# A quarter of the columns ahead in a Householder loop, side work laid out anew: a subspace rotation followed by a DiT block

## The chip, the cores and the metric

The kernel runs on one core of one Trainium2 chip, in fp32 throughout. The metric is the device time of one execution in microseconds (us); the time of a kernel is the median of several runs. Times inside an execution come from one profiled execution, counted from the start of its span. Engines are named as the profile names them: PE is TensorE's matmul (PEld its weight load), DVE is VectorE, ACT ScalarE, POOL GpSimd, SP SyncE, which issues most DMAs.

## The reference

The kernel computes two layers. The first rotates every token inside a 64-dimensional subspace; the second is a DiT block. With batch 8, 512 tokens of width 576:

```
U, _ = qr(P)                                   # P is 576 x 64, U has orthonormal columns
v = silu(cond) @ W.T + b                       # 2016 entries per batch element
A = skew(v);  R = expm(A)                      # 8 matrices of 64 x 64
z = x @ U
x = x + (z @ R - z) @ U.T                      # the rotation

ada = silu(cond) @ ada_w + ada_b               # shifts, scales, gates: 6 x 576 per batch element
x = x + gate_msa * attention(modulate(layernorm(x), shift_msa, scale_msa))   # 16 heads, over heads of one token
x = x + gate_mlp * mlp(modulate(layernorm(x), shift_mlp, scale_mlp))         # 576 -> 2304 -> gelu -> 576
```

Only what comes before the first token matters here: the QR of P, the matrices expm(A), and the products for `ada`.

## The kernel before

**The whole.** The kernel starts with a prologue of about 240 us and then runs the tokens in blocks of 128 through rotation, qkv, attention, projection and MLP for the remaining 1900 us, which this change doesn't touch. The prologue factors P by Householder reflections. Once the 64 reflections are known, the code after the loop (from L571) forms v^T v (`vv`, L577), inverts a triangular 64x64 matrix by levels (`p1`, `p2t`), and makes from that U, U^T and the first rotated block of tokens. All of that needs the whole factorization, and the blocks of tokens need it too.

**The matrix.** P lies in SBUF as `m`, 128 partitions x 5 row blocks x 64 columns; row j of the matrix (j below 64) is partition j of block 0. Step j works on the n = 64 - j columns from j on; n is how this text counts steps, 64 for the first one, 1 for the last.

**One step (`qr_step`, `column_products`).** The work of a step alternates between TensorE, ScalarE and VectorE:

- `rp` (L274): a TensorE product with a broadcast column of the identity copies row j of the matrix to all partitions. It reads row j of all remaining columns, so it needs all of the previous step's update.
- `dp` (L282): a product with a matrix of ones sums `t` over the partitions: the dot products of column j with each remaining column. `t` (L268) are sums over the five row blocks of the products `pr` (L263), made by the previous step.
- VectorE: `sg` (L291) is 0 or -2 by the sign of the diagonal entry in `rp`; `off` (L292) clears row j's place in `m`; `row` (L295) is (sg + 1) times row j. ScalarE: `nrm` (L298) is the root of column j's dot product, `nsg` (L299) is sg + 1.
- `w` (L320) = row x nrm - dp; `den` (L323) = (nrm - row_j) x nrm; `r` (L335) is its reciprocal; `up` (L327) is column j times `w`; `m` (L337) adds r x up. Then `pr` and `t` for the next step.
- `finish` makes `av` = nrm - row_j (L306), `vmax`, the largest entry of column j (L307), and `dg`, the diagonal correction (L310). The correction itself (L311) is put into the next step by `done`.

The instructions `up`, `m`, `pr` and `t` are cut into two halves of the columns (`halves`, h=0 and h=1) as long as at least 16 columns are left, in the order pr0, pr1, t0, t1.

**The side work (`beside`, L528).** After each step from the third on, one piece of other work is put into the engines' streams. The pieces come from generators:

- `skew_entries` (L399): 8 groups of 5 matmuls, the entries of A; with `paced(4, ...)` four matmuls a step. Then A is written to DRAM and read back as matrices (`skew_rows`).
- `modulations` (L517): 9 groups of 5 matmuls of `ada` (`ada_columns`, L360, six passes for three of them), and after four of the groups a `modulation` (L371), 10 or 12 small passes. `paced(3, ...)` makes it three a step.
- `expm` (L445): the products of a Taylor series in A (at, aa, ss, sss, hic, hin, sn), then 19 squarings (L503), each of two 16-pass products `pe` and `pf` of 64x64 matrices (the last has one only), a copy on ScalarE and an addition on POOL (L513); its result is `fmi` (L515).

In `beside` each yield of `expm` says whether the step is free: then three more matmuls of `ada` go with it. A squaring says False, so a pair has its step to itself. By this, skew lies at n=60 to 51, `ada` with the head of expm from there to n=34, the squarings at n=33 to 16 and nothing of it from n=15 on.

**What sets the order.** PE, DVE, ACT and POOL run in the order in which the code issues (`manual_schedule`, L164); the program compiled from it holds that order[...]. The first load of `aw`, the weights of `ada`, are four groups deep (bufs=4); later groups are loaded when an earlier one has been used. The gates of the block are stored to DRAM (`gates_d`) when groups 4 and 8 are done.

## Time and profile before

| what | value |
|---|---|
| three runs | 2156.01, 2156.08, 2163.45 us; median 2156.08 |
| profiled execution | 2157.38 us, its span 2155.7 us |
| granted TensorE clock, mean over the span | 0.962 |
| first `nrm` (n=64), `nrm` of n=40, n=22, n=4 | 7.2, 93.8, 154.9, 202.5 us |
| last diagonal correction, `vv` | 210.4, 210.6 us |
| store of the first rotated rows | 233.8 us |
| from one `nrm` to the next, us | n=64: 3.90; n=60: 4.50; n=55: 3.40; n=50: 3.27; n=46: 3.11; n=45: 4.33; n=40: 4.67; n=34: 2.97; n=24: 2.91; n=16: 2.91; n=10: 2.45; n=3: 2.30 |
| `nrm`, `nsg` on ScalarE | 0.26, 0.28 us |
| `rp`, `dp` result, at full clock (n=48) | 0.42, 0.39 us |

How to read the page and the views: the busy table gives for each engine its busy time and the share of the span. The page's digits cut the span into 40 slices of 53.9 us, each digit the busy tenths of its slice; the row PEclk gives in the same way the clock that TensorE was granted. A timeline line has the start, the duration, engine, line of code, operation, names of output and inputs, shapes, and a count when equal neighbours are put together. A busy-time-by-stretch line has the stretch and its length, then for PE, PEld, DVE, ACT and POOL the busy time with the number of instructions, then the granted clock, the DMA share and GB/s.

### The profile page before, as it was taken

Reading aid. Unit: us, or ns where it says so; the run is one execution under the profiler, and the core shown is the slowest. Engines: PE = TensorE matmul, PEld = TensorE weight load, DVE = VectorE, ACT = ScalarE, POOL = GpSimd, SP = SyncE. Lnnn points to the kernel's source line nnn. Section 1 sums busy time; section 2 is a strip of 40 time slices with the busy share of each in tenths; the row PEclk is TensorE's granted clock in tenths of the full one; section 3 lists DMA queues with packets and bytes.
Section 4 is the critical chain, followed back from the end, with each engine's and each line's share of the span. In section 5 each row is a group of like instructions: output and inputs, shape, how many; then the busy total and the mean of one; then the engine's idle time right before and its main releaser. Section 6 shows DMA issues by size and latency. Waiting matters only on the chain.

```text
span 2155.7 us, 28203 instructions
## 1 busy us (share of the span) xinstructions
PE 2052.0 (95%) x10091; PEld 1622.7 (75%) x10091; DVE 1818.0 (84%) x2544; ACT 433.6 (20%) x1040; POOL 731.8 (34%) x959
## 2 busy tenths in 40 slices
PE   6996998999999999999999999999999999999988
PEld 3475666777878888787878787888878778787867
DVE  8998499799997988979797979797988998986920
ACT  2232121212111111221121212111221121112110
POOL 2341143241523333333333242423333443343422
PEclk9965799999999999999999999999999999999989
DMA  8202265385857666565758484857667666665744
GB/s 278 87 2 75 85 209 164 114 234 161 225 178 223 194 191 222 174 217 178 234 143 271 133 266 127 244 176 210 213 180 234 187 210 182 200 189 193 218 129 131
DMA packets 251456, 392.44 MB, mean 182 GB/s; under 512 B 86926, under 2 KB 139099, under 8 KB 251316
## 3 DMA queue, kind: packets, MB, share of 16 engines
q1 hardware_dynamic: 225396, 364.09, 55.3%
q10 hardware_dynamic: 25920, 26.55, 3.6%
q8 instruction: 80, 1.31, 0.2%
q14 instruction: 60, 0.49, 0.1%
HBM read 331.63 MB, written 58.94 MB: 181 GB/s over the span
## 4 chain that ended last, share of the span: by engine, by line
PE 77%; DVE 12%; issue 3%; DMA 3%; POOL 3%; ACT 1%; ACTq 0%; SPq 0%; POOLq 0%; DVEq 0%
PE fc L993 25%; PE qkvp L821 17%; PE fc L1067 9%; PE pj L949 6%; PE fc L1072 6%; PE p L1097 3%; PE fc L1069 3%; DVE sc L866 2%; DVE qk L859 1%; DVE pv L887 1%; PE zps L751 1%; DVE att L894 1%; PE rot L762 1%; PE dp L282 1%; PE htr L794 1%
## 5 line engine op out<-in xcount | busy, mean ns | idle before, releaser
L993 PE MATMUL fc<-h2T,w 128*128 128x256 f32 x2304 | 521.1, 382 | 3.3 <-ACT h2T L969 2.1
L821 PE MATMUL qkvp<-wqkv,hT 128*128 128x288 f32 (+1 forms) x1920 | 486.5, 410 | 8.6 <-ACT qs L832 6.4
L993 PEld LDWEIGHTS fc<-h2T,w 128*128 128x128 f32 x2304 | 434.7, 191 | 71.7 <-ACT h2T L969 9.1
L821 PEld LDWEIGHTS qkvp<-wqkv,hT 128*128 128x128 f32 (+1 forms) x1920 | 364.3, 192 | 111.4 <-ACT qs L832 8.2
L859 DVE TENSOR_TENSOR qk<-qkv 128x2304 f32<-128x2304 f32 x128 | 336.8, 2631 | 15.3 <-DMA qkv<-tok 11.1
L887 DVE TENSOR_TENSOR pv<-sc,qkv 128x2304 f32<-128x2304 f32 x128 | 332.5, 2598 | 2.7
L894 DVE TENSOR_REDUCE att<-pv 128x144 f32<-128x2304 f32 x128 | 325.9, 2546 | 3.1
L866 DVE TENSOR_REDUCE sc<-qk 128x64 f32<-128x2304 f32 x128 | 326.0, 2547 | 2.5
L1092 POOL TENSOR_TENSOR s<-gt 128x128 f32<-128x128 f32 x144 | 93.5, 651 | 461.8 <-ACT gt L1014 461.8
L1014 ACT ACTIVATE gt<-fc,b 128x256 f32<-128x256 f32 x288 | 118.9, 472 | 604.5 <-PE fc L993 570.1
L1067 PE MATMUL fc<-wq,gt 128*128 128x288 f32 x576 | 170.5, 416 | 10.1 <-ACT gt L1014 7.5
L1072 PEld LDWEIGHTS fc<-wt,ss 128*128 128x128 f32 x1152 | 160.6, 190 | 15.1
L1072 PE MATMUL fc<-wt,ss 128*128 128x144 f32 x1152 | 164.7, 286 | 0.0
L832 ACT COPY qs<-qkvp 128x288 f32<-128x288 f32 x180 | 71.7, 398 | 377.0 <-PE qkvp L821 325.0
L1025 POOL TENSOR_TENSOR x<-x,mt 128x288 f32<-128x288 f32 x64 | 71.3, 1114 | 221.7 <-DVE mt L1024 221.7
L1089 POOL TENSOR_TENSOR ss<-gt 128x128 f32<-128x128 f32 x144 | 121.1, 841 | 65.1 <-PE fc L1072 65.0
L1091 POOL TENSOR_TENSOR ss<-gt,ss 128x128 f32<-128x128 f32 x144 | 130.5, 907 | 10.0
L1067 PEld LDWEIGHTS fc<-wq,gt 128*128 128x128 f32 x576 | 99.4, 190 | 44.5 <-issue 15.9
L949 PE MATMUL pj<-w2q_p,aT 128*128 128x288 f32 x384 | 105.2, 410 | 0.8 <-DVE u L1117 0.8
L146 POOL TENSOR_TENSOR rstd_m<-rstd_m,mhalf 128x1 f32<-128x1 f32 x32 | 24.5, 764 | 224.5 <-DVE rstd_m L145 224.5
L1067 PE MATMUL fc<-wt,gt 128*128 128x288 f32 x288 | 93.5, 406 | 0.0
L1069 PE MATMUL fc<-wq,ss 128*128 128x288 f32 x288 | 93.4, 406 | 0.0
(262 smaller groups left out, 2371.5 us busy)
## 6 DMA issues: line engine op xcount, KB each, us to landing
w<-in_fc_w SPq DMA_DIRECT2D x288, 256.0 KB, 5.0
wq<-in_fc_q SPq DMA_DIRECT2D x144, 432.0 KB, 4.3
wt<-comb_d SPq DMA_DIRECT2D x144, 432.0 KB, 5.9
tok<-qs ACTq DMA_DIRECT2D x180, 144.0 KB, 1.8
qkv<-tok SPq DMA_DIRECT2D x30, 864.0 KB, 4.6
w2q_p<-in_proj_w SPq DMA_DIRECT2D x32, 432.0 KB, 4.1
xT<-in_x_t SPq DMA_DIRECT2D x16, 640.0 KB, 4.8
w1t<-in_fc_t SPq DMA_DIRECT2D x80, 128.0 KB, 4.4
```

What stands on the lines that cost most here:

```text
L821: nc.tensor.matmul(ps, lhsT=hT[0:k, c, i * 128 : (i + 1) * 128], rhs=wqkv[0:k, c, cols], start=c == 0, stop=c == NK - 1,)
L859: nc.vector.tensor_tensor(pr, q[:, c * HC : (c + 1) * HC].unsqueeze(2).to_broadcast([128, HC, H, DH]), k.unsqueeze(1).to_broadcast([128, H ...
L866: nc.vector.tensor_reduce(sc[t][:, c * HC : (c + 1) * HC, :], pr, AX.X, ALU.add)
L887: nc.vector.tensor_tensor(pr, sc[t][:, c * HC : (c + 1) * HC, :].unsqueeze(2).to_broadcast([128, HC, DH, H]), v.unsqueeze(1).to_broadcast( ...
L894: nc.vector.tensor_reduce(att[:, c * HC : (c + 1) * HC, :], pr, AX.X, ALU.add)
L949: nc.tensor.matmul(ps, lhsT=aT[0:k, c, :], rhs=w, start=c == 0, stop=c == NK - 1)
L993: nc.tensor.matmul(bank[:, k], lhsT=lhs, rhs=h2T[rows, c, 0 : NU * 128], start=start, stop=stop, skip_group_check=True)
L1067: nc.tensor.matmul(p[k], lhsT=whole[k][0], rhs=whole[k][1], start=g == 0, stop=stop)
L1069: nc.tensor.matmul(p[2], lhsT=whole[2][0], rhs=whole[2][1], start=g == 0, stop=stop)
L1072: nc.tensor.matmul(bank[:, side], lhsT=lhs, rhs=rhs[:, n * QUARTER : (n + 1) * QUARTER], start=False, stop=stop, skip_group_check=True,)
L1089: nc.gpsimd.tensor_tensor(ss[:, 0], gt[:, 0, 1], gt[:, 1, 1], ALU.add)
L1091: nc.gpsimd.tensor_tensor(ss[:, 2], gt[:, 1, 0], ss[:, 1], ALU.subtract)
```

## The change

The change rewrites the step and its order, and lays out the side work anew. In words:

1. `halves` becomes `split`: the first quarter of the columns from lo on, then the other three quarters (one part if fewer than 16 are left). Each part has tiles of its own for `t` and for `dp` (`t0`, `t1`, `dp0`, `dp1`), so `dp` is two matmuls in a two-part step; the tile `dp1` takes one more PSUM bank.
2. The order of VectorE in a step: sg, row, off, w of the first part, w of the second, both `up`, r, m of the first part, vmax, pr of the first, m of the second, t of the first, pr and t of the second.
3. `av` is made by ScalarE, from row_j with `nrm` as bias and scale -1. In steps whose next one has two parts, `den` is made by ScalarE too, from `av` with `nrm` as scale. `nsg` goes.
4. `sg` and `av` of each step are kept as columns of `sgs` and `avs`; the corrections of the diagonal are made by three VectorE operations after the last step, in place of `dg` and the correction in each.
5. `skew_entries` is paced by two a step rather than four; `ada` by two a step for five steps, then with each yield of `expm` one, or two where it is free and its number is odd. A squaring now has one `ada` matmul (or a modulation) with it. In the compiled order: skew at n=60 to 41, two `ada` each at n=40 to 36, the head of expm with one or two at n=35 to 23, the squarings with one each at n=22 to 5, the last single product at n=4, the last `ada` at n=2. The second store of the gates is issued on SP behind the last group's copy, so at the end of the loop, and the loads issued behind it on that queue (weights of the sums, of fc1 and of the projection) come after it.

```diff
@@ -243,32 +243,33 @@
         vmax = prep.tile([128, R], F32, tag="vmax", name="vmax")
-
-        def halves(lo):
-            n = R - lo
-            if n < 16:
-                return [(lo, R)]
-            return [(lo, lo + n // 2), (lo + n // 2, R)]
+        avs = prep.tile([128, R], F32, tag="avs", name="avs")
+        sgs = prep.tile([128, R], F32, tag="sgs", name="sgs")
+        def split(lo):
+            first = lo + (R - lo) // 4
+            return [(lo, R)] if R - lo < 16 else [(lo, first), (first, R)]
         def wide(n):
             return [128, NK, n]
-        def column_products(j):
-
-            t = qrs.tile([128, R], F32, tag="t", name=f"t_{j}")
-            prods = []
-            for h, (a, b) in enumerate(halves(j)):
-                pr = qrs.tile(wide(R), F32, tag=f"pr{h}", name=f"pr_{j}_{h}", bufs=1)
-                nc.vector.tensor_tensor(
-                    pr[:, :, a:b], m[:, :, a:b], m[:, :, j : j + 1].to_broadcast(wide(b - a)), ALU.mult
-                )
-                prods.append(pr)
-            for pr, (a, b) in zip(prods, halves(j)):
-                nc.vector.tensor_reduce(t[:, a:b], pr[:, :, a:b].rearrange("p c i -> p i c"), AX.X, ALU.add)
+        def product(j, k, a, b):
+            pr = qrs.tile(wide(R), F32, tag=f"pr{k}", name=f"pr_{j}_{k}", bufs=1)
+            nc.vector.tensor_tensor(pr[:, :, a:b], m[:, :, a:b], m[:, :, j : j + 1].to_broadcast(wide(b - a)), ALU.mult)
+            return pr
+        def summed(j, k, a, b, pr):
+            t = qrs.tile([128, R], F32, tag=f"t{k}", name=f"t_{j}_{k}")
+            nc.vector.tensor_reduce(t[:, a:b], pr[:, :, a:b].rearrange("p c i -> p i c"), AX.X, ALU.add)
             return t
-        def qr_step(j, t, done):
+        def qr_step(j, ts):
             rp = ps_qr.tile([128, R], F32, tag="rp", name=f"rp_{j}")
             nc.tensor.matmul(
@@ -278,66 +279,75 @@
                 start=True,
                 stop=True,
             )
-            dp = ps_qr.tile([128, R], F32, tag="dp", name=f"dp_{j}")
-            nc.tensor.matmul(dp[:, j:R], lhsT=ones, rhs=t[:, j:R], start=True, stop=True)
-
-            def small(tag):
-                return qrs.tile([128, 1], F32, tag=tag, name=f"{tag}_{j}")
+            dps = []
+            for k, (t, (a, b)) in enumerate(zip(ts, split(j))):
+                dp = ps_qr.tile([128, R], F32, tag=f"dp{k}", name=f"dp_{j}_{k}")
+                nc.tensor.matmul(dp[:, a:b], lhsT=ones, rhs=t[:, a:b], start=True, stop=True)
+                dps.append(dp)
+            def small(tag, n=1):
+                return qrs.tile([128, n], F32, tag=tag, name=f"{tag}_{j}")
             n = R - j
-            row, sg, nsg, nrm, av = (small(x) if x != "row" else None for x in ("row", "sg", "nsg", "nrm", "av"))
-            row = qrs.tile([128, R], F32, tag="row", name=f"row_{j}")
+            row, nrm, den, r = small("row", R), small("nrm"), small("den"), small("r")
+            sg, av = sgs[:, j : j + 1], avs[:, j : j + 1]
             nc.vector.tensor_scalar(sg, rp[:, j : j + 1], 0.0, -2.0, ALU.is_ge, ALU.mult)
+            nc.vector.scalar_tensor_tensor(
+                row[:, j:R], sg.to_broadcast([128, n]), 1.0, rp[:, j:R], ALU.add, ALU.mult
+            )
             nc.vector.tensor_tensor(
                 m[:, 0, j:R], m[:, 0, j:R], off[:, j : j + 1].to_broadcast([128, n]), ALU.mult
             )
-            nc.vector.scalar_tensor_tensor(
-                row[:, j:R], sg.to_broadcast([128, n]), 1.0, rp[:, j:R], ALU.add, ALU.mult
-            )
-            nc.scalar.activation(nrm, dp[:, j : j + 1], AF.Sqrt, bias=tiny)
-            nc.scalar.activation(nsg, sg, AF.Identity, bias=ones[:, 0:1])
-            if done:
-                done()
-
-            def finish():
-
-                dg = small("dg")
-                nc.vector.tensor_scalar(av, nrm, row[:, j : j + 1], None, ALU.subtract)
+            nc.scalar.activation(nrm, dps[0][:, j : j + 1], AF.Sqrt, bias=tiny)
+            nc.scalar.activation(av, row[:, j : j + 1], AF.Identity, bias=nrm, scale=-1.0)
+            def largest():
                 nc.vector.tensor_reduce(
                     vmax[:, j : j + 1], m[:, :, j], AX.X, ALU.max, apply_absolute_value=True
                 )
-                nc.vector.tensor_scalar(dg, ident[:, j : j + 1], av, nsg, ALU.mult, ALU.mult)
-                return lambda: nc.vector.tensor_tensor(
-                    m[:, 0, j : j + 1], m[:, 0, j : j + 1], dg, ALU.subtract
-                )
-
+            cols = split(j + 1)
+            if len(cols) == 1:
+                largest()
             if j + 1 == R:
-                return None, finish()
-
-            w = qrs.tile([128, R], F32, tag="w", name=f"w_{j}")
-            den, r = small("den"), small("r")
-            nc.vector.scalar_tensor_tensor(
-                w[:, j + 1 : R], row[:, j + 1 : R], nrm, dp[:, j + 1 : R], ALU.mult, ALU.subtract
-            )
-            nc.vector.tensor_scalar(den, nrm, row[:, j : j + 1], nrm, ALU.subtract, ALU.mult)
-            outer = []
-            for h, (a, b) in enumerate(halves(j + 1)):
-                up = qrs.tile(wide(R), F32, tag=f"up{h}", name=f"up_{j}_{h}", bufs=1)
+                return None
+            if len(cols) == 1:
+                nc.vector.tensor_scalar(den, nrm, row[:, j : j + 1], nrm, ALU.subtract, ALU.mult)
+            else:
+                nc.scalar.activation(den, av, AF.Identity, scale=nrm)
+            w = small("w", R)
+            for dp, (a, b) in zip(dps, split(j)):
+                a = max(a, j + 1)
+                if a < b:
+                    nc.vector.scalar_tensor_tensor(w[:, a:b], row[:, a:b], nrm, dp[:, a:b], ALU.mult, ALU.subtract)
+            def outer(k, a, b):
+                up = qrs.tile(wide(R), F32, tag=f"up{k}", name=f"up_{j}_{k}", bufs=1)
                 nc.vector.tensor_tensor(
                     up[:, :, a:b],
                     m[:, :, j : j + 1].to_broadcast(wide(b - a)),
                     w[:, a:b].unsqueeze(1).to_broadcast(wide(b - a)),
                     ALU.mult,
                 )
-                outer.append(up)
-                if h == 0:
-                    nc.vector.reciprocal(r, den)
-            for up, (a, b) in zip(outer, halves(j + 1)):
-                nc.vector.scalar_tensor_tensor(
-                    m[:, :, a:b], up[:, :, a:b], r, m[:, :, a:b], ALU.mult, ALU.add
-                )
-            return column_products(j + 1), finish()
+                return up
+            def update(up, a, b):
+                nc.vector.scalar_tensor_tensor(m[:, :, a:b], up[:, :, a:b], r, m[:, :, a:b], ALU.mult, ALU.add)
+            ups = [outer(k, *ab) for k, ab in enumerate(cols)]
+            nc.vector.reciprocal(r, den)
+            update(ups[0], *cols[0])
+            if len(cols) == 2:
+                largest()
+            pr = product(j + 1, 0, *cols[0])
+            if len(cols) == 2:
+                update(ups[1], *cols[1])
+            ts = [summed(j + 1, 0, *cols[0], pr)]
+            if len(cols) == 2:
+                ts.append(summed(j + 1, 1, *cols[1], product(j + 1, 1, *cols[1])))
+            return ts
         def paced(n, parts):
@@ -528,14 +538,15 @@
         def beside():
             yield
             yield
-            yield from paced(4, [skew_entries(g) for g in range(8)])
+            yield from paced(2, [skew_entries(g) for g in range(8)])
             skew_rows()
-            rest = paced(3, [modulations()])
-            for _ in range(4):
+            rest = modulations()
+            for _ in range(5):
+                next(rest)
                 next(rest)
                 yield
-            for free in expm(*eyes):
-                if free:
+            for k, free in enumerate(expm(*eyes)):
+                for _ in range(2 if free and k % 2 else 1):
                     next(rest, None)
                 yield
             for _ in rest:
@@ -551,9 +562,9 @@
         first_xt = xin.tile([128, D], F32, tag="xt", name="xt_0_0", bufs=2)
         eyes = identities()
         side = beside()
-        t, done = column_products(0), None
+        ts = [summed(0, k, a, b, product(0, k, a, b)) for k, (a, b) in enumerate(split(0))]
         for j in range(R):
-            t, done = qr_step(j, t, done)
+            ts = qr_step(j, ts)
             if j > 1:
                 next(side, None)
             if j == 30:
@@ -569,7 +580,10 @@
         if True:
-            done()
+            dg = prep.tile([128, R], F32, tag="dg", name="dg")
+            nc.vector.scalar_tensor_tensor(dg, sgs, 1.0, avs, ALU.add, ALU.mult)
+            nc.vector.tensor_tensor(dg, dg, ident[:, 0:R], ALU.mult)
+            nc.vector.tensor_tensor(m[:, 0, :], m[:, 0, :], dg, ALU.subtract)
             below = ps_ex.tile([R, 1], F32, tag="ex", name="below")
             nc.tensor.matmul(below, lhsT=vmax, rhs=ones[:, 0:1], start=True, stop=True)
             vv = ps_qr.tile([R, R], F32, tag="rp", name="vv")
...
-                p1 = ps_qr.tile([R, R], F32, tag="dp", name=f"p1_{s}")
+                p1 = ps_qr.tile([R, R], F32, tag="dp0", name=f"p1_{s}")
```

## The prediction

> **What bounds the kernel now.** First the head of the page. The profiled execution took 2157.38 us for a span of 2155.7 (1.7 outside), 1.3 above the median of 2156.08, so a difference worked out in the trace is set against the median unchanged.
>
> ```profile
> span 2155.7 us, 28203 instructions
> PE 2052.0 (95%) x10091; PEld 1622.7 (75%) x10091; DVE 1818.0 (84%) x2544; ACT 433.6 (20%) x1040; POOL 731.8 (34%) x959
> DVE  8998499799997988979797979797988998986920
> PEclk9965799999999999999999999999999999999989
> ```
>
> PE is busy 95% of the span, but the change touches only the first 210 us (slices 1 to 4). There DVE's digits are 8 and 9 and TensorE's clock falls to 6 and 5. The starts of `nrm` (L298) give the stages, n being the columns left in a step: first `nrm` 7.2, n=40 at 93.8, n=22 at 154.9, n=4 at 202.5, last diagonal correction 210.6. Call them A (n=64 to 41, 86.5 us), B (40 to 23, 61.2), C (22 to 5, 47.6) and D (8.0). What follows hangs on the factorization, so its end moves the whole. Next, busy time by stretch (length, then busy time of PE, PEld, DVE, ACT, POOL, granted clock, DMA):
>
> ```profile
> 40.00:60.00 20.00, 15.58 (x70) 7.20 (x70) 19.44 (x109) 4.29 (x17) 0.00 (x0) 1.00 0.38 114
> 120.00:140.00 20.00, 17.86 (x220) 16.28 (x220) 19.34 (x115) 7.13 (x24) 7.72 (x11) 0.58 0.01 2
> 140.00:160.00 20.00, 20.00 (x252) 18.77 (x251) 19.75 (x126) 8.20 (x28) 9.37 (x15) 0.50 0.01 2
> 180.00:210.00 30.00, 14.02 (x50) 12.43 (x50) 25.45 (x176) 5.76 (x26) 0.00 (x0) 0.50 0.39 133
> ```
>
> DVE looks like the bound everywhere, at 94 to 99%. But at 140 to 160, in the expm squarings, PE is 20.00 of 20 as well, at half clock, and after 180 it has the most room: the side work is already done. The timeline shows one step of each sort.
>
> ```profile
> 64.23 0.20 DVE L306 TENSOR_SCALAR av<-nrm,row 128x1 f32<-128x1 f32 x1
> 64.35 0.15 DVE L307 TENSOR_REDUCE vmax<-m 128x1 f32<-128x5 f32 x1
> 64.54 0.27 DVE L310 TENSOR_SCALAR dg<-ident,av,nsg 128x1 f32<-128x1 f32 x1
> 64.73 0.15 DVE L291 TENSOR_SCALAR sg<-rp 128x1 f32<-128x1 f32 x1
> 64.78 2.10 PE L364 MATMUL ada<-aw,sc 128*8 128x384 f32 x6
> 65.03 0.15 DVE L311 TENSOR_TENSOR m<-m,dg 128x1 f32<-128x1 f32 x1
> 65.24 0.26 DVE L320 SCALAR_TENSOR_TENSOR w<-row,nrm,dp 128x47 f32<-128x47 f32 x1
> 65.42 0.27 DVE L323 TENSOR_SCALAR den<-nrm,row 128x1 f32<-128x1 f32 x1
> 65.60 0.27 DVE L327 TENSOR_TENSOR up<-m,w 128x115 f32<-128x115 f32 x1
> ...
> 78.72 3.78 PE L364 MATMUL ada<-aw,sc 128*8 128x384 f32 x6
> ...
> 127.38 0.60 PE L282 MATMUL dp<-t,ones 128*128 128x31 f32 x2
> 127.91 1.12 PE L429 MATMUL pe<-ex_e,ex_f 64*64 64x64 f32 x16
> 128.82 1.06 PE L429 MATMUL pf<-ex_f,ex_e 64*64 64x64 f32 x16
> 129.81 0.63 PE L274 MATMUL rp<-m,ident 128*128 128x30 f32 x2
> ```
>
> At n=48 DVE's instructions start without a hole, every 0.12 to 0.2 us. At n=31 PE starts the next thing the moment the last is out: rp 0.45, dp 0.52, two products 1.9, together the step's 2.9. Three ada matmuls (six passes) take 2.10 at full clock, 3.78 at half: 0.70 or 1.26 each.
>
> **DVE's saving.** Removed from a step: av (0.12 from its start to the next), dg 0.19, the m-dg correction 0.21, den 0.18: 0.70. Given back: a second w 0.14; row right behind sg, on which it depends, 0.19 rather than 0.07; w behind off with waits for ScalarE and TensorE, 0.23 rather than 0.12; r to m 0.19 rather than 0.07; pr1 to t1 in sequence +0.13: about 0.6. Net gain at n=48: 0.1 us. At full clock that is 24 x 0.1 = 2.4 in A. At half clock another loop is longer: t1, dp1 (0.11 to get going, 0.63 for its result), second w, up, m, pr, t1, about 3.3 against 3.2: a loss of 0.1. So -0.1 to +0.1 a step. Beside a POOL addition the correction took 0.56 (at 127.93) rather than 0.15, so its removal may save 0.4 more in a squaring step; PE's queue hides that there, and I take 0. The deferred diagonal is three instructions, about 0.3 at the end, for the one correction of before. The moved vmax waits for nothing new: 0. The fourth PSUM tile (dp1) is only space: 0.
>
> Does the quarter run ahead? rp, first in PE's queue, still needs row j of all columns, so the late three quarters' update; dp0 stands behind rp. The chain from that update's end, at full clock: rp 0.11 + 0.26, dp0 0.39, nrm 0.06 + 0.26, handover 0.03 = 1.1 us; beneath it t0, pr1, t1, sg, row, off, about 1.3. So nrm stops being late, but gets no earlier than DVE's packing allows.
>
> **ScalarE's den.** nrm's end + 0.03, av 0.284 (its nearest row is nsg, L299), 0.035, den 0.284 to 0.377 (like nsg, or with one more pointer): 0.63 to 0.73 until r may start. Beneath it DVE has two w and two up, 0.6 to 0.8 down to n=40, less after: 0 above, 0.06 to 0.13 a step at n=24 to 16, at most 1.5. Here a rule speaks against the change: the Trainium skill, "ScalarE: Activation LUTs", "Rules for kernel authors", gives multiply and add to VectorE. By duration the row agrees (0.284 against den's 0.27 and av's 0.20), so the rule's sum would be +0.7 a step on 48 steps, 34 us; but DVE's rows stand without holes and ScalarE is busy 4.29 of 20, so I take the cover, 0 to +1.5, value +0.5.
>
> **PE's side work.** This is the large term. The change moves no product off PE; it adds a dp1 in 49 steps (0.52 at half, 0.33 at full clock), and lays the same 40 skew and 45 ada matmuls and four modulations out anew: two skew a step over 20 steps (before: four over ten), then two ada a step, one or two beside the expm head, and one ada beside each pair of squarings at n=22 to 5. Before, the pairs had steps of 2.9 us (n=33 to 16) to themselves, and n=15 to 1, where PE was under half busy, had nothing. Add PE's own occupancy:
>
> A at half clock: two skew 2 x 0.88 (eight passes took 3.53 at 22.46) and 1.49 of rp and dps = 3.25, just DVE's 3.3. From nrm to nrm, n=60 and 59 took 4.50 and 4.28 in before, n=45 to 41 (three ada each) 19.2 together: at 3.4 and 3.3 a step that is -1.9 and -2.7, and the other 19 lose 0.13 each, +2.5: -2. At full clock -1.9, -3.8 (3.1 a step) and 19 x -0.1: -7.5.
>
> B, n=40 to 23: 18 x 1.49, 26 ada x 1.26 = 32.8, seven products x 0.95, 20 modulation passes x 0.22: 70.7 us at half clock, and 2 to 4 for the head's waits (each product needs a copy on ScalarE), against 61.2: +12. At full clock PE has 18 x 0.92 + 26 x 0.70 + 4.2 + 2.4 = 41, so DVE bounds: 18 steps of 3.0 (n=38 and 34, with little beside them, took 2.90 and 2.97) and 2 of waits, 56: -5.
>
> C, n=22 to 5: 18 x 0.97, dp1 7 x 0.52, pairs 18 x 1.9, 16 ada x 1.26, two modulations of 2.64: 80.8 us at half clock against 47.6: +33. At full clock (rp and dps 0.59 and 0.92, pair 1.15, ada 0.70, modulations 1.4) about 47.8, nothing.
>
> D: the late ada at n=4 to 2 and the three diagonal instructions, +0.9.
>
> All at half clock: -2 + 12 + 33 + 1 = +44 (2200); all at full: -7.5 - 5 + 0 + 1 = -11.5 (2144.5). Nothing covers this sum: at half clock PE is the bound, and DVE waits at sg for an rp that queues behind the ada. SP: the last gate store now waits for the last ada copy at the end, with the weight loads (about 9 us of issue, at 179 to 188 in before) behind it; their first user, the store of the first rotated rows, comes 23 us after the end of the factorization. I count 0, at worst +2.
>
> **Which clock.** Here the trace and a rule part. The Trainium skill, "TensorE: Matmul & The Clock Gate", "What's actually happening", lets the clock rise after one window of about 3.4 us of sustained work, and fall only after an idle one; by it, with PE never idle, the change would give the full-clock sum, -11.5. The row speaks against: at 140 to 160 PE is busy 20.00 of 20 and granted 0.50. Busy in the profile isn't enough; what held full clock in before was the dense ada bursts (6 passes of 384 columns in a row, 60 to 80: 0.97), and with the small 64x64 squarings it fell to 0.58 and 0.50. One ada beside a pair is between: per 3.4 us about 1500 to 1800 streamed columns, where the stretches of before that stayed half lie under some 1600 and those that rose near 1790. I take A at half most of the time (-2), B three quarters half (+8), C half of the steps half (+16.5), D +0.9: **+23**, 2179.
>
> **The rivals.** (1) Likeliest: PE becomes the bound, clock mixed: 2167 to 2191, 57%. (2) The same with half clock throughout: 2192 to 2202, 18%. For it: 0.50 over the squarings; against: the ada do stream. (3) On the other side: the evenly laid ada keep the clock full from about n=60 on, then PE holds 41 of 56 us in B and DVE's small saving shows: -3 to -11.5, 2144.5 to 2153, 10%. It decides if B and C are at full clock for over eight tenths: each tenth of them at half costs (17 + 33)/10 = 5. (4) Nearly balanced, full clock for most of C: 2153 to 2167, 15%. A rival to the means: the quarter never gets ahead, as dp0 stays behind rp; that leaves DVE's packing as counted and is inside each case (2154 if it were all). ScalarE's den binding as well gives 2156.
>
> **The numbers.** Likeliest 2179. The range 2156 to 2201 leaves out case 3, the lowest of case 4 and the highest of case 2. By over 0.5% (about what a measurement of this kernel tells from no change, 2145.3 and 2166.9) faster: half of case 3, 5%; within: its other half and nearly all of 4, 19%; slower: 76%.
>
> **What would show it.** Right: the busy table has PE at 19 to 20 of 20 from n=40 on down to n=5, with the side work ending near n=2, not n=15; steps of n=22 to 16 of 3.5 to 4.6 us rather than 2.9; sg's idle time ended by rp; DVE's instructions down by three in a two-part step. Wrong: granted clock 1.00 through n=22 to 5, PE under 90% there, steps of 2.6 or less; or den releasing r late in most steps. It would also be wrong if the wait moves past the factorization, to the loads behind the gate store.

## The result and the profile after

The changed kernel takes 2169.82 us (median of five runs, 2168.60 to 2175.22) against 2156.08: 1.0062 times the kernel before, 95% interval 1.0047 to 1.0078, so 13.7 us slower where the prediction had 23 and a range of 2156 to 2201. The profiled execution is the slowest of the five, 2175.22 us, 17.8 above the profiled execution of before, so about 4 us of what the stages below show is not in the medians. The page's head answers to the lines shown of before:

```profile
span 2173.5 us, 28188 instructions
PE 2089.4 (96%) x10189; PEld 1636.0 (75%) x10189; DVE 1807.9 (83%) x2356; ACT 454.9 (21%) x1088; POOL 735.1 (34%) x959
DVE  8967399799999897979797979798897999886930
PEclk9968599999999999999999999999999999999999
```

PE got 37 us busier and DVE 10 less; the digits of DVE fall to 6, 7 and 3 in slices 3 to 5, where before had 9, 8 and 4. From the starts of `nrm`, read off the timeline:

| stage | before, us | after, us | measured | predicted |
|---|---|---|---|---|
| start of the first `nrm` | 7.2 | 6.4 | -0.9 | |
| A, n=64 to 41 | 86.5 | 83.1 | -3.4 | -2 |
| B, n=40 to 23 | 61.2 | 67.7 | +6.5 | +8 |
| C, n=22 to 5 | 47.6 | 61.4 | +13.8 | +16.5 |
| n=4 to `vv` | 8.1 | 9.6 | +1.5 | +0.9 |

`vv` starts at 228.06 rather than 210.60 (+17.5), and the store of the first rotated rows is issued at 251.26 rather than 233.81 (+17.5): nothing was added or won back behind the loop. Busy time by stretch, with the columns as before:

```profile
40.00:60.00 20.00, 19.56 (x59) 10.37 (x57) 18.78 (x88) 5.33 (x20) 0.00 (x0) 1.00 0.32 108
120.00:140.00 20.00, 19.41 (x86) 12.10 (x84) 12.81 (x63) 5.39 (x19) 14.10 (x19) 0.50 0.15 46
140.00:160.00 20.00, 17.69 (x124) 10.27 (x125) 14.73 (x87) 7.46 (x24) 4.61 (x7) 0.67 0.27 89
180.00:210.00 30.00, 27.34 (x389) 19.36 (x388) 23.14 (x111) 13.78 (x42) 13.92 (x21) 0.93 0.01 2
```

At 120 to 140 DVE is no longer full (12.81 of 20; before had 19.34) and PE is. Who waits for whom is in the list of VectorE's waits (us in total, times, longest), first of before over n=40 to 1, then of after over the same steps:

```profile
DVE w L320 <- ACT nrm L298: 3.0, 14, 0.2
DVE sg L291 <- PE rp L274: 2.2, 3, 1.0
...
```

```profile
DVE sgs L295 <- PE rp L275: 26.9, 20, 3.1
DVE den L317 <- ACT nrm L302: 2.4, 9, 0.3
DVE w L324 <- ACT nrm L302: 1.5, 7, 0.2
...
```

`sg` waited for `rp` 2.2 us in before and 26.9 now. The timeline of TensorE shows four skew passes of stage A, four ada passes at full clock, and then a whole step at half clock with what stands ahead of `rp`:

```profile
21.95 1.85 PE L415 MATMUL skew<-wr,sc 128*8 128x252 f32 x4
...
93.17 1.46 PE L374 MATMUL ada<-aw,sc 128*8 128x384 f32 x4
...
126.14 0.63 PE L275 MATMUL rp<-m,ident 128*128 128x30 f32 x2
126.58 1.03 PE L285 MATMUL dp<-t,ones 128*128 128x7 f32 x4
127.54 1.12 PE L439 MATMUL sss<-ex_s,ex_s 64*64 64x64 f32 x16
128.59 2.73 PE L374 MATMUL ada<-aw,sc 128*8 128x384 f32 x4
131.25 0.63 PE L275 MATMUL rp<-m,ident 128*128 128x29 f32 x2
```

From one rp to the next PE has no gap: 5.1 us for a step (n=30) that took 3.3 in before. The first line is a warning about the clock column. It reads 1.00 in the stretch 40 to 60, but two skew matmuls (four passes) take 1.85 there as at 21.95, and in before eight passes took 1.87 at 34.67, at full clock; the first change that the clock's record holds is a rise at 92.3, and ahead of it the column shows 1.00 by default. The durations say that stage A ran at half clock. (In before the record begins with a rise at 30.9; before's skew passes ahead of it are as slow, eight in 3.53 us.) After A the record has full clock for 20 of B's 68 us (30%) and for 38 of C's 61 (61%); the prediction had a quarter and a half.

### The profile page after: what moved, and what is told of

Read it like the earlier page. It is cut to its first block, busy times and chain, and to the rows that moved or that the text cites. A ratio compares the mean times of both kernels' runs of the same rounds, so it can differ in the third digit from the quotient of the medians.

```text
span 2173.5 us, 28188 instructions
## 1 busy us (share of the span) xinstructions
PE 2089.4 (96%) x10189; PEld 1636.0 (75%) x10189; DVE 1807.9 (83%) x2356; ACT 454.9 (21%) x1088; POOL 735.1 (34%) x959
## 4 chain that ended last, share of the span: by engine, by line
PE 74%; DVE 16%; issue 3%; POOL 3%; DMA 2%; ACT 1%; SPq 0%; ACTq 0%; POOLq 0%; DVEq 0%
PE fc L1007 23%; PE qkvp L835 15%; PE fc L1081 8%; PE fc L1086 5%; PE pj L963 5%; DVE sc L880 3%; DVE qk L873 3%; PE fc L1083 3%; PE p L1111 3%; PE dp L285 2%; DVE pv L901 2%; DVE att L908 2%; PE ada L374 1%; PE rp L275 1%; PE rot L776 1%
## 5 line engine op out<-in xcount | busy, mean ns | idle before, releaser
L1105 POOL TENSOR_TENSOR ss<-gt,ss 128x128 f32<-128x128 f32 x144 | 137.3, 953 | 10.0
```

The source lines that it names most:

```text
L1105: nc.gpsimd.tensor_tensor(ss[:, 2], gt[:, 1, 0], ss[:, 1], ALU.subtract)
```

## Experiments

All times are medians of runs of the kernel and of the kernel before on the same chip, taken in turn. The kernel before had 2156.0 on the first chip (qr_only to den_dve), 2161.1 on the second (no_ada_sq to diag_end), 2155.6 on the third (the dense kernels) and, on that same chip later, 2163.0 (clock_fill), so differences are compared, not times. Stage times come from one profiled execution of each kernel.

**qr_only: the new step with the old layout.** Only `beside` is the old one:

```diff
-            yield from paced(2, [skew_entries(g) for g in range(8)])
+            yield from paced(4, [skew_entries(g) for g in range(8)])
...
-            rest = modulations()
+            rest = paced(3, [modulations()])
```

> The new Householder step (quarter ahead, two dp, av and den on ScalarE, diagonal at the end) with the old layout of the side work. Theory (TensorE becomes the bound through the new layout; the new step itself saves 0.1 us on VectorE and costs a second dp on TensorE): the squarings stand alone again at n=33 to 16, where the second dp adds about 0.5 us to a step of 2.9 at half clock, +8; the stretch with three ada a step adds 13 x 0.33 = 4; the first steps save 2: 2161 to 2167. Rival (the layout is innocent, the new step is what costs, for instance by ScalarE's den): as the changed kernel, 2168 to 2172. Second rival (the new step is a plain gain): 2150 to 2154.

Measured: 2164.65, +8.7 (1.0045, interval 1.0032 to 1.0059), as the theory had it. The squarings, on PE:

```profile
140.45 0.63 PE L275 MATMUL rp<-m,ident 128*128 128x27 f32 x2
140.89 1.02 PE L285 MATMUL dp<-t,ones 128*128 128x6 f32 x4
141.84 1.12 PE L439 MATMUL pe<-ex_e,ex_f 64*64 64x64 f32 x16
142.75 1.06 PE L439 MATMUL pf<-ex_f,ex_e 64*64 64x64 f32 x16
143.75 0.62 PE L275 MATMUL rp<-m,ident 128*128 128x26 f32 x2
```

These steps last 3.30 us each, 2.90 in before: the second dp costs 0.40 where PE is the bound (0.52 was taken). At n=58 to 49, both kernels at full clock, a step takes 3.29 on average against 3.35: VectorE's gain is 0.06 where 0.1 was counted. At n=14 to 5 it takes 0.10 more than before.

**side_only: the old step with the new layout.** The `beside` of the change in the kernel before; nothing else.

> The old Householder step with the new layout of the side work. Theory: the cost of the changed kernel less the second dp in the steps that TensorE bounds (about 24 of them at 0.4): 2160 to 2166, with sg waiting for rp over n=40 to 5 as in the changed kernel. Rival (the new step is what costs): 2154 to 2158.

Measured: 2167.14, +11.1 (1.0048, 1.0033 to 1.0064), at the upper end of the theory's range and a little past it. sg's waits over n=40 to 1:

```profile
DVE sg L291 <- PE rp L274: 15.9, 14, 2.6
...
```

B is 3.4 longer than in before and C 14.4. The layout alone makes PE the bound, and most of its price lies in C. The two parts of the change don't add (8.7 and 11.1 against 13.7 together). A count of the steps says why, though no run tests it: in qr_only all 18 squarings stand at n=33 to 16, where `dp` has two parts, but the layout moves them to n=22 to 5, where only the seven down to n=16 have a second `dp` to pay for.

**one_dp: the changed kernel with one dp a step** (and one tile t for both parts).

```diff
-            for k, (t, (a, b)) in enumerate(zip(ts, split(j))):
...
-                nc.tensor.matmul(dp[:, a:b], lhsT=ones, rhs=t[:, a:b], start=True, stop=True)
+            nc.tensor.matmul(dp[:, j:R], lhsT=ones, rhs=ts[0][:, j:R], start=True, stop=True)
```

> The changed kernel with one tile t and one dp matmul a step; VectorE keeps its two parts and their order. nrm then waits for all of t. Theory: 24 TensorE-bound steps lose 0.3 to 0.5 each, so 8 to 10 faster than the changed kernel, 2160 to 2163. Rival (the bound of those steps is the chain of ScalarE or POOL, or the early dp is what holds the step together): no faster, or slower by up to 0.3 a step in the early steps, 2168 to 2180.

Measured: 2187.62, +31.6 (1.0146, 1.0129 to 1.0163), 18 worse than the change. This was the rival's way, but beyond its 2180: 0.5 a step where it had said 0.3 (n=58 to 49: 3.98 against 3.48, both at half clock). The timeline of one step:

```profile
55.04 0.48 DVE L272 TENSOR_REDUCE t<-pr 128x39 f32<-128x195 f32 x1
55.44 0.15 DVE L297 TENSOR_SCALAR sgs<-rp 128x1 f32<-128x1 f32 x1
55.62 0.21 DVE L298 SCALAR_TENSOR_TENSOR row<-sgs,rp 128x52 f32<-128x52 f32 x1
55.66 0.64 PE L287 MATMUL dp<-t,ones 128*128 128x52 f32 x2 [0.38 <-DVE sgs L297]
55.74 0.20 DVE L301 TENSOR_TENSOR m<-m,off 128x52 f32<-128x52 f32 x1
56.34 0.26 ACT L304 ACTIVATE nrm<-dp,tiny 128x1 f32<-128x1 f32 x1 [2.67 <-PE dp L287]
56.64 0.39 DVE L326 SCALAR_TENSOR_TENSOR w<-row,nrm,dp 128x12 f32<-128x12 f32 x2 [0.69 <-ACT nrm L304]
```

From the end of `t` (55.52) to `w` (56.64) are 1.1 us of dp and nrm, and only sg, row and off are left to lie beneath. In the kernel before av, vmax, dg and the correction lay there too. So the early dp0 is not an extra: it is what the step needs once those four are gone. What the run tests is the split of `t` and `dp` in two; whether a quarter is better than a half was not tested.

**den_dve: den on VectorE,** in every step, and behind `w` (in the one-part steps the change has it on VectorE ahead of `w`).

```diff
-                nc.scalar.activation(den, av, AF.Identity, scale=nrm)
+                nc.vector.tensor_scalar(den, nrm, row[:, j : j + 1], nrm, ALU.subtract, ALU.mult)
```

> The changed kernel with den made by VectorE in every step, as before the change; av stays on ScalarE, off the path. Theory (ScalarE's den is covered; VectorE has slack from n=40 on, and is about level with TensorE before): 24 early steps get 0 to 0.15 longer, 2170 to 2173. Rival (the two ScalarE operations in a row bind r): 1.5 to 4 faster than the changed kernel, 2166 to 2168.

Measured: +20.2 (1.0088, 1.0075 to 1.0101), some 6.5 more than the change, beyond the 0 to 3 of the theory and away from the rival: ScalarE's den doesn't bind (`r` has no wait for it in the changed kernel's list), and VectorE's den costs. The two profiles are 4.1 apart at `vv`: A +2.5 (0.1 a step), B +2.9, C -0.9, the first step -0.3; the rest of the 6.5 stays open. In B four steps at n=40 to 37 take 4.0 to 4.1 each: the clock first rises at 107.6, not at 92.3. That second part is the clock's, not den's; the next run shows the same shift in a program that is the change's up to there. The last steps test the order: n=3 and 2 take 2.32 each here, 2.38 and 2.37 in the change and 2.30 in before.

**no_ada_sq: the last 20 ada left out.** A modified changed kernel in which groups 5 to 8 are a constant.

```diff
+            if g >= 5:
+                for c in range(NK):
+                    yield
+                nc.gpsimd.memset(ada_rows[:, g * AC : (g + 1) * AC], 0.5)
...
+                return
```

> The changed kernel with the last four groups of ada (5 to 8) left out, so that the squarings at n=22 to 5 stand alone; the two modulations among them stay and read a constant. It leaves out that part of the computation. By TensorE's own sum at half clock those steps take 6 x 3.3 + 12 x 2.9 + two modulations 5 = 60 us, against the 61.4 that the changed kernel took with its clock full for 61% of the stretch: if the clock is lost with the ada, hardly a gain, 2166 to 2170. If instead the ada beside the squarings are the price, and the clock stays as it was, 16 ada at 0.9 = 14 are gained: 2154 to 2158.

Measured: +14.7 (1.0072, 1.0055 to 1.0088), no gain at all on the change's +13.7. Busy time by stretch:

```profile
160.00:180.00 20.00, 18.56 (x202) 17.68 (x202) 13.67 (x75) 7.98 (x27) 7.39 (x11) 0.50 0.01 2
180.00:200.00 20.00, 19.95 (x251) 18.71 (x251) 16.29 (x77) 8.80 (x28) 8.82 (x13) 0.50 0.01 2
200.00:220.00 20.00, 19.41 (x228) 18.19 (x226) 11.51 (x67) 7.88 (x26) 8.87 (x13) 0.50 0.00 1
```

PE is as full as with the ada, at half clock throughout (0.93 over 180 to 210 in the changed kernel). C took 61.9 us, against 61.4 with them and 60 by the sum on record; the two modulations wait 2.0 for POOL's constant, which the other kernels don't have, and without that C would be at the 60 of the sum. The 16 ada of C, some 14 us at 0.9, thus cost next to nothing: they pay for themselves through the clock. In B, whose program is that of the change, the clock rose at 105.0 and B took 70.1 rather than 67.7: some us of difference between executions come from where the clock's windows fall.

**tail_ada and tail_ada_new: thinner ada, the rest in the last steps**, with the old and with the new step.

```diff
-            rest = paced(3, [modulations()])
+            rest = modulations()
...
                 if free:
                     next(rest, None)
+                    next(rest, None)
```

> The old step; skew at four a step and squarings alone at n=33 to 15 as before the change, but only two ada beside each free step of the head of expm rather than three, and the last 13 in the steps from n=14 on, one a step. Theory: in those last steps TensorE waits 1.3 to 1.5 us before each rp, so an ada of 1.26 costs nothing even at half clock; the stalls of 12 us at n=45 to 33 shrink if the clock stays full there: 2147 to 2154. If thinner ada lose the clock there, 2154 to 2160. Rival (work beside the last steps is in their chain): 2160 to 2170.

> The new step with the layout of tail_ada. Theory: as the new step with the old layout (2164.7), less what that layout gains, 2 to 8: 2157 to 2163. Rival (the new step needs the even layout of the change to pay): 2166 to 2172.

Measured: +0.1 (1.0003, 0.9993 to 1.0013) and +12.6 (1.0051, 1.0033 to 1.0069; its ratio corresponds to 11). The first shows both halves of the theory at once. In the last steps the ada is free: n=14 to 8 take 2.61 to 2.41 as in before, since an ada of 1.45 ends just where rp becomes possible:

```profile
188.33 0.57 PE L282 MATMUL dp<-t,ones 128*128 128x11 f32 x2
188.84 1.45 PE L364 MATMUL ada<-aw,sc 128*8 128x384 f32 x2
190.22 0.60 PE L274 MATMUL rp<-m,ident 128*128 128x10 f32 x2
```

And with two ada a step the clock is half for most of the head, 0.61 at 80 to 100 and 0.56 at 100 to 120, where before had 0.84 and 0.85; n=44 to 42 take 5.0 on average. What the thinner ada saved, the clock took (+0.1 was within the second range of the theory). The second kernel was expected 1 to 7 above the 2156 of before and came out in the rival's span, 10 to 16 above, though not for the rival's reason: it lost the clock as well (mostly half from 77 on), and its squarings take the 3.30 us of qr_only.

**diag_end: the diagonal at the end, alone** (the three operations behind the loop are added as in the change).

```diff
-                nc.vector.tensor_scalar(dg, ident[:, j : j + 1], av, nsg, ALU.mult, ALU.mult)
-                return lambda: nc.vector.tensor_tensor(m[:, 0, j : j + 1], m[:, 0, j : j + 1], dg, ALU.subtract)
```

> The old step and the old layout, with one part of the change alone: the diagonal corrections at the end (two VectorE instructions and nsg less a step, three at the end); av stays on VectorE. Theory: VectorE's instructions between t and w also cover the way t, dp, nrm; taking 0.4 of them away leaves 0.15 to gain in some 30 steps at full clock, nothing beside the squarings and nothing in the last steps: 2151 to 2155. Rival (VectorE's packing is the bound of every step outside the squarings): 47 x 0.4 = 19 faster, 2137. Rival (the cover is needed in full): 2155 to 2158.

Measured: -0.4 (0.9995, 0.9981 to 1.0008), which is the last rival's figure (the theory's would have been 1 to 5 faster). Its steps at n=58 to 49 are 0.05 us shorter than before's (3.30, all at full clock in both), 0 from n=26 on. All of the new step together had gained 0.06 there.

**dense_tail, dense_late, dense_late_diag: keep the ada dense, and put what is left into the last steps.** dense_tail keeps three a step for 36 pieces and puts the last 13 into the last steps. dense_late also moves the modulations there, each in two halves:

```diff
-                v = {1: 0, 2: 1, 5: 3, 7: 4}.get(g)
-                if v is not None:
-                    modulation(v)
-                    yield
+            for v in (0, 1, 3, 4):
+                yield from modulation(v)
...
+            dense = 9
...
-                if free:
-                    next(rest, None)
+                if free and dense:
+                    dense -= 1
+                    for _ in range(3):
+                        next(rest, None)
```

> The old step; three ada a step as before the change for the first 36 pieces (to n=38), none beside the last four free steps of the head of expm, and the last 13 pieces one a step from n=14 on. Theory (full clock needs about three ada a step; the last steps take one for nothing): n=46 to 38 as before, n=37 to 33 some 3 us shorter, the modulation in a last step +0.7: 2 to 4 faster than before. Rival (any ada moved out of the head costs as much clock as it saves, as with two a step): within 1 of before.

> The old step; 39 ada at three a step to n=37, the other six and all four modulations, each cut in two, one a step from n=14 on. The modulations' many small passes no longer stand among the ada. Theory (the half-clock windows at n=45, 40 and 36 of before follow the modulations, which stream next to nothing): the clock stays full to about n=36 and n=45 to 34 go from 46.4 us to about 38 to 41; the last steps gain 0 to 2: 4 to 8 faster than before. Rival (those dips come from the products of expm, not from the modulations): 1 to 3 faster.

> dense_late with the diagonal corrections at the end, as in diag_end, whose early steps were 0.05 us shorter. Theory: 1 to 2 faster than dense_late. Rival (no difference, as in the medians of diag_end): within 1 of dense_late.

Measured: -0.4 (0.9999, 0.9987 to 1.0012), -5.5 (0.9975, 0.9967 to 0.9983) and -10.6 (0.9953, 0.9935 to 0.9971; 2145.04 us). dense_tail is its rival's case. dense_late is the theory's: with the modulations gone the clock is full without a break from 27 to 105 us.

```profile
80.00:100.00 20.00, 17.79 (x108) 7.79 (x108) 19.38 (x104) 5.23 (x19) 14.33 (x19) 1.00 0.28 89
100.00:120.00 20.00, 12.41 (x130) 10.44 (x130) 18.96 (x110) 4.61 (x18) 6.66 (x10) 0.63 0.01 2
```

n=45 to 34 take 41.9 us (38 to 41 expected), 46.4 in before, and the squarings and the modulations in the last steps cost nothing. dense_late_diag is faster than dense_late by more than its step explains (expected 1 to 2; medians and profiled spans differ by 5, but in the profiles `nrm` of n=1 starts only 1.8 earlier). The rest lies behind the loop, where the two profiles have the clock at half for 41.7 and 28.1 us; why it differs there stays open. dense_late_diag is faster than both kernels; of the 12.6 us by which its profile is shorter than before's, 7.5 are there at `vv`.

**clock_fill: add work to hold the clock.** `filler(n, cols)` is n matmuls of `ones` with cols columns of the qkv weights.

```diff
...
+                elif k > 12:
+                    filler(1)
...
+            for k in range(14):
+                next(rest, None)
+                filler(1, 384 if k < 6 else 512)
+                yield
```

> dense_late_diag with work added: from n=36 on each step also gets one wide matmul (384 or 512 columns, as an ada; two or three in the free steps of the head), whose result nobody reads. It adds some 45 of them, 0.70 to 0.93 us each at full clock, 1.26 to 1.7 at half, all in steps where TensorE at full clock has 1 us or more to spare. Theory (the clock follows the columns streamed per 3.4 us): the clock stays full past 105 us, the squarings keep 2.8 to 2.9 (POOL's and ScalarE's chain), the last steps lose 0.2 each at rp and at dp, 2.0 to 2.2 in place of 2.3 to 2.6: 3 to 8 faster than dense_late_diag, about 2138 to 2142 where before takes 2156. If the clock falls in the head and does not come back, 19 x 1.26 of TensorE's time are added to the squarings: 15 to 30 slower than dense_late_diag. Rival (the clock has nothing to do with the kind of work): the second outcome.

Measured: +12.1 (1.0056, 1.0036 to 1.0075), so some 23 slower than dense_late_diag, where the theory had 3 to 8 faster. That is the figure set down for a lost clock, but the clock did what the theory said: full from 31 to 201 us, but for 10. At n=14 to 8 the steps are 0.22 shorter than dense_late_diag's. The time did not follow. The squarings took 3.5 to 3.8 us at full clock (up to 4.2 where it dipped, at n=28 and 27), with PE idle ahead of dp:

```profile
121.39 1.02 DVE L334 SCALAR_TENSOR_TENSOR m<-up,r,m 128x75 f32<-128x75 f32 x2
121.58 0.72 POOL L513 TENSOR_TENSOR ex_f<-ex_f,ex_i 128x256 f32<-128x256 f32 x1 [2.40 <-PE pe L429]
122.26 0.72 POOL L513 TENSOR_TENSOR ex_e<-ex_e,ex_i 128x256 f32<-128x256 f32 x1
122.33 0.91 DVE L267 TENSOR_TENSOR pr<-m 128x75 f32<-128x75 f32 x2
122.46 0.41 PE L278 MATMUL rp<-m,ident 128*128 128x31 f32 x2 [0.19 <-DVE m L334]
123.76 0.38 PE L286 MATMUL dp<-t,ones 128*128 128x31 f32 x2 [0.89 <-DVE t L272]
```

With the products done early, POOL's two additions come while VectorE updates m and forms pr: 1.02 and 0.91 us for pairs that take 0.49 and 0.37 in before. That is 1.1 us a step, of which 0.8 shows in the step at n=31 (3.78 against 2.94 in dense_late_diag). From n=7 on the modulations, with a filler each, lost the clock again, and six steps of 3.0 to 4.0 followed.

## Why the prediction was right, and where it wasn't

**PE becomes the bound: right, and shown, for the steps at half clock.** It needed two things, the layout (side_only +11.1) and the second dp (qr_only +8.7, 0.40 a squaring step). Where PE is the bound the sum of its occupancies gives the steps: at half clock n=17 is 1.49 + 1.9 + 1.26 = 4.65 (measured 4.67), and the modulation at n=18 1.49 + 1.9 + 2.3 = 5.7 (5.93, with 0.3 of wait for ada's copy). Of the signs that were named, sg's wait for rp and the side work up to n=2 came. PE at 19 to 20 of 20 came at 120 to 140 only (17.69 at 140 to 160, 27.34 of 30 at 180 to 210), and of the seven steps n=22 to 16 four took over 3.5 us and three, at full clock, 2.9 to 3.1.

**The size: 23 forecast, 13.7 in the medians, 17.8 in the profiles.** The stage sums were each within 3 us of the profile; that C came so near is in part luck. Half of its 18 steps at half clock, 9 at 33/18 = 1.8 each, made the 16.5. Measured, six steps were wholly or in part at half clock (n=22, 18 to 16, 6 and 5) and cost 10.4, 1.7 each: the cost was right, their number too high. The other twelve (n=21 to 19 and 15 to 7), put at nothing, cost 3.4, 0.28 each. The two errors partly balance. By its clock C was the prediction's case 4, "full clock for most of C", and 2169.8 lies just above that case's 2167. Why full clock is not free in C shows in the timeline at n=10:

```profile
197.89 0.72 POOL L523 TENSOR_TENSOR ex_f<-ex_f,ex_i 128x256 f32<-128x256 f32 x1 [1.41 <-PE pe L439]
198.05 0.62 DVE L262 TENSOR_TENSOR pr<-m 128x50 f32<-128x50 f32 x1
```

pr takes 0.62 beside POOL's addition, 0.21 in before, and ends 0.06 after the addition does (198.67 and 198.61): +0.41, and +0.10 for the one-part steps' new order (next point), less about 0.2 for rp and dp at full clock, is about the +0.3 a step that was measured. Only the first term is read off; den_dve, with that order undone, takes 2.81 at n=14 to 8 like the change, so the other two are not separated. The prediction had seen this contention at the correction (0.56 for 0.15) and set it to nothing, because it looked at the instruction that the change removes; the addition stays and falls upon another.

**VectorE's saving: right in kind, half in size.** 0.1 a step was taken, 0.06 measured. Four instructions of 0.7 us went; that hardly a tenth of it is left has the reason that one_dp and diag_end show: they covered the way t, dp, nrm. In the last steps, counted level, the new step cost 0.10 each (qr_only, n=14 to 5): there `den` stands ahead of `w`, and both wait for nrm, as qr_only's timeline shows.

```profile
194.69 0.26 ACT L302 ACTIVATE nrm<-dp,tiny 128x1 f32<-128x1 f32 x1 [2.01 <-PE dp L285]
...
194.99 0.27 DVE L317 TENSOR_SCALAR den<-nrm,row 128x1 f32<-128x1 f32 x1 [0.24 <-ACT nrm L302]
195.18 0.21 DVE L324 SCALAR_TENSOR_TENSOR w<-row,nrm,dp 128x9 f32<-128x9 f32 x1
```

The kernel before has w directly behind nrm. den_dve, with den behind w again, gets back 0.06 and 0.05 of the 0.08 and 0.07 that n=3 and 2 had lost.

**The quarter.** The prediction said that dp0 cannot get ahead of rp, and gave the quarter no gain of its own. The first is right. But against the same step with one dp, two are worth 18 us (one_dp). What the prediction missed is that the new step cannot do without an early dp0.

**ScalarE's den: right.** It is covered; moved to VectorE it costs 0.1 a step in A. The rule that gives such work to VectorE would have been the wrong choice here, by a measured 2.5 us in A.

**The clock: the row was right, the rule wasn't.** By the rule weighed there (Trainium skill, "TensorE: Matmul & The Clock Gate", "What's actually happening") a TensorE that is never idle would have been full. no_ada_sq keeps PE at 19.95 of 20 and at 0.50. Taking wide matmuls away lost the clock (no_ada_sq), moving the modulations out from among them kept it (dense_late), and adding a wide one beside each squaring raised it (clock_fill). What counts can be read from the traces. The clock changes only in steps of 3.41 us. Take each such window and count the columns that PE's passes stream in it, each pass weighted by its rows out of 128 (the 64-row passes of the squarings start in twos, at 127.910 and 127.917 us in before). Over the 14 traces, from each one's first recorded change to 260 us, there are 853 windows. All 518 with under 1530 columns were followed by half clock, all 323 with over 1600 by full clock; the 12 between went both ways. It is a regularity of what ran; no run varied the weight by rows alone. Some of the windows:

| window | PE busy | columns | clock of the next window |
|---|---|---|---|
| before, 44.6 to 48.0 (four skew a step) | 0.78 | 1986 | 1.00 |
| before, 143.6 to 147.0 (squarings alone) | 1.00 | 1411 | 0.50 |
| tail_ada, 82.0 to 85.4 (two ada a step) | 1.00 | 1537 | 0.50 |
| after, 177.6 to 181.0 (squarings with one ada, n=17) | 1.00 | 1355 | 0.50 |
| after, 198.1 to 201.5 (squarings with one ada, n=11 and 10) | 0.91 | 2151 | 1.00 |

So busy time doesn't decide. The last two rows say why C was mixed: a squaring and its ada stream some 1850 columns a step, too few per window while the step takes the 4.67 us of half clock, enough once it takes 2.78. And two skew a step give 929 to 1344 columns a window through A (20 to 88 us), so A stayed at half. The prediction's own count, half under some 1600 and a pair with one ada at 1500 to 1800, had this nearly right, but not that a slower step thins its own stream.

**The rival on the other side**, a full clock throughout, gave 2145. It didn't occur, and its sum was too good: at 0.28 for each of 18 steps, C at full clock would have cost 5 us where it had nothing, and in clock_fill, with the old step and a nearly full clock, the squarings at n=33 to 17 took 3.5 us and more. Queue SP, the store of the gates with the loads behind it, cost nothing, as counted.

What stays open: how much of the spread of 2168.6 to 2175.2 comes from where the clock's windows fall, which programs with the same beginning suggest (first rise at 92.3 and 105.0) and no run isolates.

## What to carry to other kernels

Side work that is laid evenly beside a chain of short steps takes the slack of the engine that carries it, not that of the engine one wants to relieve: add its occupancy per step, at the clock that is in fact granted, before spreading it. An instruction taken off the busiest engine gains only what remains after the latency that it covered; ask what it stood in front of. And where the clock follows what is streamed, dense stretches with the rest put where the engine waits anyway beat an even spread: dense_late, the old step with that layout, is 0.25% faster than the kernel before where side_only, the old step with the even one, is 0.48% slower. Before adding work to raise a clock, ask what the faster engine will trigger: in clock_fill it brought POOL's additions onto VectorE's path.

## What the runs showed of the hardware

- The granted clock of a 3.41 us window followed the row-weighted columns streamed in the window before: half after fewer than 1530, full after more than 1600, in 841 of 841 windows; PE's busy share was 1.00 in many of the first kind and as low as 0.56 in the second.
- Removing 20 matmuls (no_ada_sq) shortened nothing: the clock went from 61% full to half in that stretch. Adding some 45 (clock_fill) raised the clock to full.
- VectorE's pr and m are stretched beside POOL's additions (one pr from 0.21 to 0.62 us, ending 0.06 after the addition), and a faster TensorE moves where the additions fall.
- The clock column reads 1.00 ahead of the first change in the record; up to 92 us the matmuls' durations in the changed kernel say half.
